# Turned tokens: from transposes on TensorE to a second read in turned layout, normalized in the value stage

## The chip, the cores and the metric

The kernel runs on one NeuronCore of a Trainium2 chip. A core has five engines with instruction streams of their own: TensorE (PE in the profile; its weight loads are PEld), VectorE (DVE), ScalarE (ACT), GpSimd (POOL) and SyncE (SP), which here issues nearly all DMA transfers. Each engine runs its stream in order, and engines wait for one another by semaphores. The metric is the device time of one execution in microseconds (us), lower is better; the time before is the median of three runs.

## The reference

One block of gated cross attention and a linear layer with adapters, over 32 sequences of 64 tokens of 512 elements, all in fp32 (shortened):

```python
def _layernorm(x, axis=-1, eps=1e-05):
    m = jnp.mean(x, axis=axis, keepdims=True)
    v = jnp.var(x, axis=axis, keepdims=True)
    return (x - m) / jnp.sqrt(v + eps)

# in attention: 32 heads of 128
q = (hidden_q @ Wq).reshape(b, lq, h, dh)
k = (hidden_kv @ Wk).reshape(b, lk, h, dh)
v = (hidden_kv @ Wv).reshape(b, lk, h, dh)
score = jnp.einsum('bqhd,bkhd->bhqk', q, k) * scale + position_bias
score = jnp.where(mask, score, neg_inf)
probs = jax.nn.softmax(score, axis=-1)
ctx = jnp.einsum('bhqk,bkhd->bqhd', probs, v).reshape(b, lq, h * dh)
return ctx @ Wo
...
x = x + jnp.tanh(g_xattn[0]) * attention(_layernorm(x), ctx_4096, mask, fside, Wq, Wk, Wv, Wo)
x = x + jnp.tanh(g_ffn[0]) * linear_with_adapters(_layernorm(x), ...)
```

The change touches one thing in it: `_layernorm(x)` of the first line, and the form in which it reaches the query product. That product contracts over the 512 elements, so it wants the normalized tokens turned: elements on the partitions, tokens along the free dimension.

## The kernel before

The tokens are handled in two phases (NPH = 2) of 1024 tokens (TP), each cut into NT = 8 tiles of 128 tokens and NCH = 2 halves of 512 tokens. A phase has three stages.

**Stage K** (the first loop of `stage_a`, line 619): for each of the 16 head pairs n, the product of the context with Wk. From n = 2 on, each is one `unit` (line 347): a 2 x 2 block product in seven products (p1 to p7) instead of eight, each product in three matmul passes over high and low halves of both operands (`mm3`). The operands are the high and low parts of the seven sums of blocks. For the weights `key_blocks` (line 533) makes them while the unit before runs: POOL forms sums and low parts, ACT the high parts, from `rawk`, which SP loads through `fetch`, two buffers in turn. ACT and DVE gather the products into `kT` (two buffers), and `store` sends it to DRAM (`kd`). A unit's last two products and its store are carried into the next unit.

**Stage V** (the second loop, line 661): for each of four groups g of weights and each of four token slices t, a `unit` with Wv; `store` sends the results to `vd`. The blocks of group g + 1 are made on POOL and ACT (`blocks_v`), from `wvr`, loaded at t = 1 of group g. In group 2 `turned_sums` starts, on POOL, to form the sums of the turned tokens `f`; in group 3 `turned_blocks` goes on with them.

**Attention** (`attention`, line 698) then runs over the head pairs with the query product, scores, softmax, probabilities times values, and the output product. After the second phase comes the linear layer.

The order of work is written out by hand. Side work runs in generators held in the list `streams`; `beat()` advances each by one step, and `unit` calls it after each of its seven products. `drain(g)` finishes a generator at once. Instructions go to their engines in the order in which this program reaches them. All loads and stores named here but two are on SP's queue, in order.

**The turned tokens before.** From n = 3 on `x_stats` (line 561) loads the eight token tiles (`xs`) and takes mean and variance with tokens on the partitions (bn_stats, bn_aggr); `ln_rstd` computes one over the root in small DVE steps. At n = 9 `x_turns` (line 574) starts: each tile is loaded again (`xt`), normalized on DVE (`ln_apply`, line 129: one tensor_scalar with a mean and a factor per partition), transposed on TensorE against the identity in four pieces into one PSUM buffer (`transposes`, line 132), and copied by ACT into the two tiles `f` (`x_turn`, line 520). The tiles `f` hold [128 elements, 4, 512 tokens] each, and take the slots in which the context lay. The stage ends with `drain(xturn)` and `drain(v0)`.

PSUM has eight buffers of 128 x 512 fp32 for everything. The tiles of tag "row" have two buffers of 128 x 512.

## Time and profile before

| what | value |
|---|---|
| median of three runs | 1547.89 us (1547.86 to 1548.68) |
| the profiled execution, its own time | 1547.98 us |
| its span, first to last instruction | 1545.8 us |
| granted TensorE clock, mean | 1.000 of full speed |
| stage K, first phase (0 to 162.7 us) | PE busy 161.26, DVE 98.80, ACT 78.44, POOL 120.14; DMA share 0.57 |
| stage V, first phase (162.7 to 327) | PE busy 164.30, DVE 69.16, ACT 56.54, POOL 121.84; DMA share 0.50 |
| stage K, second phase (724 to 895) | PE busy 171.00, DVE 111.82, ACT 81.18, POOL 127.94; DMA share 0.53 |
| stage V, second phase (895 to 1060) | PE busy 165.00, DVE 77.35, ACT 56.36, POOL 121.69; DMA share 0.50 |

How to read it: a busy time is the sum of an engine's instructions in the stretch; matmuls are pipelined, so that their durations overlap and a busy PE isn't PE at its peak. "DMA share" is the mean busy share of the core's 16 DMA engines. Matmuls and other groups are named by the tile they write and the tile they read, without buffer numbers ("tpx<-ident,xt"); Lnnn is a line of the kernel, often that of a helper. In a timeline the columns are start, length, engine, line, operation and tiles, and in brackets the idle time before and who ended it. The chain of work is followed back from the last instruction through whatever released each step.

### The profile page before, as it was taken

The page shows a single profiled execution, that of the slowest core. Times are in us where ns is not written, and L with a number is a line of the kernel's source. Part 1 is how long each engine was busy: PE and PEld are TensorE (multiplying, and loading weights), DVE is VectorE, ACT ScalarE, POOL GpSimd, SP SyncE. Part 2 cuts the span into 40 slices and gives each one's busy share as a digit, 9 for nine tenths or more (in the row PEclk, how much of TensorE's full clock was granted, in tenths as well). Part 3 has the DMA queues.
Part 4 walks back from the last instruction along what each step waited for, and adds up shares of the span by engine and source line. Part 5 has one row for each costly group of instructions (what it writes and reads, how often), then busy time and mean ns, then how long its engine had stood idle before and what let it go on. Part 6 is the DMA issues. An engine that isn't in the chain of part 4 may idle for free.

```text
span 1545.8 us, 24999 instructions
## 1 busy us (share of the span) xinstructions
PE 1538.4 (100%) x9080; PEld 1295.4 (84%) x9080; DVE 946.5 (61%) x1579; ACT 728.6 (47%) x1605; POOL 1015.8 (66%) x1128
## 2 busy tenths in 40 slices
PE   9999999999999999999999999999999999999999
PEld 7888888888888888888888888888888888888887
DVE  5675343377676757575686536437666676757763
ACT  6354233345555555556435423334555555555620
POOL 3898378967665757575589837896666665757410
PEclk9999999999999999999999999999999999999999
DMA  6654444374243424441565544438424342544201
GB/s 211 239 191 177 167 169 163 137 280 177 83 177 137 167 85 176 187 150 65 215 213 191 177 170 165 164 136 290 167 85 176 137 175 84 179 182 161 68 35 67
DMA packets 80989, 246.37 MB, mean 159 GB/s; under 512 B 9857, under 2 KB 10881, under 8 KB 72674
## 3 DMA queue, kind: packets, MB, share of 16 engines
q1 hardware_dynamic: 80578, 244.26, 43.9%
q8 instruction: 71, 1.16, 0.3%
q10 hardware_dynamic: 288, 0.52, 0.1%
q14 instruction: 52, 0.43, 0.1%
HBM read 171.35 MB, written 73.40 MB: 158 GB/s over the span
## 4 chain that ended last, share of the span: by engine, by line
PE 96%; DMA 2%; DVE 2%; issue 0%; ACT 0%; POOL 0%; SPq 0%; DVEq 0%; ACTq 0%; POOLq 0%
PE pa L96 22%; PE po L817 7%; PE pzv L96 6%; PE pvv L96 6%; PE pxv L96 6%; PE pzq L96 5%; PE pxq L96 5%; PE pxk L96 5%; PE pzk L96 5%; PE pvk L96 5%; PE pvq L96 5%; PE ps L759 4%; PE pf L96 4%; PE ppk L96 3%; PE pyv L96 3%; PE pyk L96 2%
## 5 line engine op out<-in xcount | busy, mean ns | idle before, releaser
L96 PE MATMUL pa<-wo,ch 128*128 128x512 f32 x1024 | 319.9, 393 | 0.0
L792 ACT COPY pt<-tp 32x256 f32<-32x256 f32 x496 | 200.3, 404 | 87.3 <-DVE tp L775 76.2
L88 POOL TENSOR_TENSOR wo<-rawo,wo 128x512 fp32r<-128x512 f32 x64 | 81.2, 1288 | 223.1 <-ACT wo L87 215.3
L96 PEld LDWEIGHTS pa<-wo,ch 128*128 128x128 f32 x1024 | 189.4, 188 | 40.0
L841 DVE TENSOR_TENSOR acc<-pa,acc 128x512 f32<-128x512 f32 x256 | 170.0, 673 | 79.5 <-PE pa L96 79.3
L96 PE MATMUL pa<-wo,cl 128*128 128x512 f32 x512 | 199.7, 390 | 0.0
L817 PEld LDWEIGHTS po<-pt,v 128*128 128x128 f32 x1024 | 119.1, 192 | 2.6 <-ACT pt L792 0.2
L821 DVE TENSOR_TENSOR cl<-po,ch 128x512 fp32r<-128x512 f32 x128 | 88.3, 691 | 51.9 <-ACT ch L820 51.4
L817 PE MATMUL po<-pt,v 128*128 128x128 f32 x1024 | 119.4, 275 | 0.0
L352 DVE TENSOR_TENSOR vt<-pvv,vt 128x512 f32<-128x512 f32 x64 | 44.1, 689 | 113.3 <-PE pvv L96 113.3
L96 PEld LDWEIGHTS pa<-wo,cl 128*128 128x128 f32 x512 | 96.1, 188 | 20.7
L820 ACT CAST ch<-po 128x512 fp32r<-128x512 f32 x128 | 75.0, 586 | 72.0 <-PE po L817 71.4
L765 ACT ACTIVATE sm<-sm 128x512 f32<-128x512 f32 x64 | 40.5, 633 | 122.7 <-POOL sm L764 122.7
L764 POOL TENSOR_TENSOR sm<-sm,mx 128x512 f32<-128x512 f32 x64 | 66.9, 1048 | 45.6 <-DVE mx L763 45.6
L374 ACT COPY vt<-pxv 128x512 f32<-128x512 f32 x32 | 18.8, 588 | 132.7 <-PE pxv L96 132.7
L352 DVE TENSOR_TENSOR kT<-pvk,kT 128x512 f32<-128x512 f32 x56 | 38.5, 688 | 69.4 <-PE pvk L96 68.8
L720 POOL TENSOR_TENSOR sm<-sm,madd 128x512 f32<-128x512 f32 x60 | 76.4, 1296 | 2.7 <-DMA sm<-bias 2.7
L783 POOL TENSOR_TENSOR sm<-sm,r 128x512 f32<-128x512 f32 x64 | 66.9, 1045 | 14.5 <-DVE r L782 11.1
L759 PE MATMUL ps<-kB,qT 128*64 128x64 f32 x2048 | 67.2, 224 | 0.3 <-DVE qT L352 0.3
L352 DVE TENSOR_TENSOR qT<-pzq,qT 128x512 f32<-128x512 f32 x64 | 44.2, 691 | 38.0 <-PE pzq L96 37.6
L352 DVE TENSOR_TENSOR vt<-pzv,vt 128x512 f32<-128x512 f32 x64 | 44.2, 691 | 37.1 <-PE pzv L96 36.9
L759 PEld LDWEIGHTS ps<-kB,qT 128*64 128x64 f32 x2048 | 62.5, 138 | 4.9 <-issue 0.7
(976 smaller groups left out, 3706.2 us busy)
## 6 DMA issues: line engine op xcount, KB each, us to landing
kd<-kT SPq DMA_DIRECT2D x64, 512.0 KB, 3.2
vd<-vt SPq DMA_DIRECT2D x128, 256.0 KB, 2.3
kB<-kd SPq DMA_DIRECT2D x32, 1024.0 KB, 4.9
v<-vd SPq DMA_DIRECT2D x32, 1024.0 KB, 8.7
rawq<-wq SPq DMA_DIRECT2D x32, 512.0 KB, 4.1
sm<-bias SPq DMA_DIRECT2D x64, 256.0 KB, 5.3
rawo<-wo SPq DMA_DIRECT2D x32, 512.0 KB, 3.5
rawk<-wk SPq DMA_DIRECT2D x31, 512.0 KB, 5.6
```

Of the source, the lines that this page charges most:

```text
L88: eng.tensor_tensor(lo, raw, hi.bitcast(F32), ALU.subtract)
L96: nc.tensor.matmul(ps, a, b, start=start and i == 0, stop=stop and i == 3 * n - 1, skip_group_check=True)
L352: nc.vector.tensor_tensor(o, ps, i, ALU.add)
L720: nc.gpsimd.tensor_tensor(t, t, masks[p][0], ALU.add)
L759: nc.tensor.matmul(ps[h * S:(h + 1) * S, t, :], qT[:, i, tok], kT[:, i, tok], start=True, stop=True)
L764: nc.gpsimd.tensor_tensor(s, s, mx.unsqueeze(2).to_broadcast([P, NT, S]), ALU.subtract)
L783: nc.gpsimd.tensor_tensor(ss[i], ss[i], r.unsqueeze(2).to_broadcast([P, NT, S]), ALU.mult)
L792: f(pt[dst, i, :, src], of[src, :, ki * 32:(ki + 1) * 32])
L817: nc.tensor.matmul(ps[:, t * P:(t + 1) * P], b["v", n // 2][c][:, t, hg * P:(hg + 1) * P], pt[:, i, c * 4 + t, :], start=True, stop=True)
L820: nc.scalar.copy(ch[:, i, sl], ps)
L821: nc.vector.tensor_tensor(cl[:, i, sl], ps, ch[:, i, sl].bitcast(F32), ALU.subtract)
L841: nc.vector.tensor_tensor(acc[t], ps, acc[t], ALU.add)
```

## The change

The host hands over a second copy of x, `xT`, in turned layout (per half of 512 tokens and quarter of 128 elements, [128 elements, 512 tokens]). Stage K reads it at n = 3 straight into `f`: eight loads of 256 KB, issued ahead of the first loads of wv. `x_turns` and `x_turn` go, with their second load of the token tiles, their normalizations on DVE, their transposes on TensorE and their copies on ACT.

The statistics are computed as before, with tokens on the partitions. In turned layout the mean and the factor of a token must stand on every partition, in the token's column. So `x_spread`, at n = 10, writes the 1024 means and the 1024 factors to DRAM (`lnd`), token by token, by two DMAs whose innermost runs on the DRAM side are single elements of 4 bytes; and `x_norm`, a stream of stage V's first group, reads them back as rows of 512 spread over all 128 partitions (`partition_broadcast`), two rows for each half, and subtracts and multiplies in place: 16 tensor_tensor of 128 x 512 on DVE in each phase, one per beat. It is drained when group 1 begins. The statistics are drained at n = 10 instead of n = 9.

```diff
@@ flamingo_block @@
+    lnd = [dram.tile([2, TP], F32, name=f"lnd{p}") for p in range(NPH)]
...
-    def x_turn(xt, f, p, t):
-        ps = transposes(xt, f"x{p}_{t}")
-        nc.scalar.copy(f[t // 4][:, :, (t % 4) * P:(t % 4 + 1) * P], ps)
...
-    def x_turns(p, f):
+    def x_spread(p):
         mv, y = mvx[p], rx[p]
-        xt = x_load(p, 0, "xt")
-        for t in range(NT):
-            nx = x_load(p, t + 1, "xt") if t + 1 < NT else None
-            for _ in range(2):
-                yield
-            ln_apply(xt, xt, mv, y, t)
+        nc.sync.dma_start(out=lnd[p][0].rearrange("(t q) -> q t", q=P), in_=mv[:, :, 0])
+        nc.sync.dma_start(out=lnd[p][1].rearrange("(t q) -> q t", q=P), in_=y)
+
+    def x_norm(p, f):
+        for j in range(NCH):
+            row = [rows.tile([P, 512], F32, tag="row", name=f"ln{p}_{j}_{i}") for i in range(2)]
+            for i in range(2):
+                nc.sync.dma_start(out=row[i], in_=lnd[p][i][j * 512:(j + 1) * 512].partition_broadcast(P))
             for _ in range(3):
                 yield
-            x_turn(xt, f, p, t)
-            xt = nx
-            yield
+            for op, r in ((ALU.subtract, row[0]), (ALU.mult, row[1])):
+                for kt in range(KT):
+                    nc.vector.tensor_tensor(f[j][:, kt, :], f[j][:, kt, :], r, op)
+                    yield
...
             if n == 3:
                 f = [big(f"f{j}", [P, KT, 512], F32, f"xf{p}_{j}") for j in range(2)]
+                for j in range(NCH):
+                    for kt in range(KT):
+                        nc.sync.dma_start(out=f[j][:, kt, :], in_=xT[p * NCH + j, kt])
...
-            if n == 9:
+            if n == 10:
                 drain(xstat)
-                xturn = x_turns(p, f)
-                streams.append(xturn)
+                x_spread(p)
...
-        drain(xturn)
         drain(v0)
+        xnorm = x_norm(p, f)
+        streams.append(xnorm)
         xq = {}
         for g in range(NG):
             if g == 1:
+                drain(xnorm)
                 streams.append(mask_stream(p))
...
         "x": C(A(x).reshape(ntok // P, P, D)),
+        "xT": C(A(x).reshape(NPH * NCH, 512, KT, P).transpose(0, 2, 3, 1)),
```

More of the change, by code (lines that the diff above doesn't have):

```diff
@@ L42, in flamingo_block @@
 @with_exitstack
-def flamingo_block(ctx: ExitStack, tc: tile.TileContext, x, ctxT, bias, mask, gx, gf,
+def flamingo_block(ctx: ExitStack, tc: tile.TileContext, x, xT, ctxT, bias, mask, gx, gf,
                    wq, wk, wv, wo, wffn, bffn, la, lb, starts, out):
```

## The prediction

> **What bounds the kernel now.** I read the page's busy times and its chain first.

> ```profile
> PE 1538.4 (100%) x9080; PEld 1295.4 (84%) x9080; DVE 946.5 (61%) x1579; ACT 728.6 (47%) x1605; POOL 1015.8 (66%) x1128
> ...
> PE 96%; DMA 2%; DVE 2%; issue 0%; ACT 0%; POOL 0%; SPq 0%; DVEq 0%; ACTq 0%; POOLq 0%
> ```

> TensorE (PE) is busy for 1538.4 of 1545.8 us and 96% of the chain. Work taken off PE shortens the time by what PE spent on it, provided that nothing newly late makes PE wait. The clock column stands at full speed throughout. Next, the instructions on the tile that the change removes:

> ```profile
> L135 PE MATMUL tpx<-ident,xt x64: 270/272/273, 100.4 to 894.0; 128*128 128x128 f32 x64
> ...
> L522 ACT COPY xf<-tpx x16: 577/587/593, 101.5 to 894.3; 128x512 f32<-128x512 f32 x16
> ```

> The 272 ns are a pipelined duration, not what a transpose takes from PE. That comes from the chain in order of time (start, length, what), where one unit starts after another:

> ```profile
> 81.49 2.72 PE pxk L96 x12
> 91.01 2.72 PE pxk L96 x12
> 100.97 2.77 PE pxk L96 x12
> ...
> 171.04 2.72 PE pxv L96 x12
> ...
> 823.79 2.72 PE pxk L96 x12
> ...
> 903.82 2.72 PE pxv L96 x12
> ```

> A unit without transposes takes 91.01-81.49 = 9.52 us. From 91.01 to 171.04 lie eight units with the eight token tiles' transposes: 80.03 us, not 8 x 9.52 = 76.16. The difference, 3.87 us (0.48 per tile), is the price; the second phase has the same 80.03 (823.79 to 903.82).

> [...] the 0.74 us POOL operation takes 1.20 beside a DVE one. [...] No store of single elements is in this trace. [...]

> **The change, part by part.**

> *Removed, stage K, each phase:* 8 x 4 transposes, 3.87 us of PE, so 7.74 us in all. Also 8 copies of 0.587 us on ACT, 8 normalizations on DVE (0.81 us) and 8 loads of 256 KB. These last three were off the chain: worth nothing by themselves.

> *Added at n = 3:* eight loads of the turned tokens, 2.1 MB, ahead of the wv loads. Eight issues of 0.44 us (four of ctx took 1.75) fit between 32.43, the end of a rawk issue, and 40.13, the next kd issue, with the four wv and two xs issues (3.2 us). The old contents of f0/f1 were last read near 24.4 us, so SP has no wait. But the data meets a full DMA:

> ```profile
> 34.00:46.50 12.50, 12.50 (x57) 10.36 (x56) 5.62 (x10) 5.31 (x15) 12.34 (x18) 1.00 1.01 375
> 103.50:109.00 5.50, 5.50 (x26) 4.51 (x25) 3.71 (x5) 2.43 (x6) 4.65 (x6) 1.00 0.07 22
> ```

> (Stretch, busy times, clock, DMA share, GB/s.) At 375 GB/s, 2.1 MB take 5.6 us; the rawk load at 41.02 lands that much later, and the key blocks behind it move:

> ```profile
> 41.02 0.71 SPq L262 DMA_DIRECT2D rawk<-wk  x1
> ...
> 47.47 0.41 ACT L293 CAST wk5p<-rawk 128x256 fp32r<-128x256 f32 x1 [0.53 <-DMA rawk<-wk]
> ...
> 53.07 0.74 POOL L297 TENSOR_TENSOR wk5p<-wsk,wk5p 128x256 fp32r<-128x256 f32 x1
> ...
> 54.40 0.66 DVE L190 TENSOR_TENSOR vs<-wvr_0a,wvr_0b 128x512 f32<-128x512 f32 x1
> ...
> 54.46 1.20 POOL L297 TENSOR_TENSOR wk5p<-wsk,wk5p 128x256 fp32r<-128x256 f32 x1
> ...
> 58.21 1.52 PE L96 MATMUL pyk<-c0p,wk5p 128*128 128x512 f32 x6
> ```

> The tightest block is p6: POOL ends its low part at 53.81, PE reads it with the third matmul of py, at 58.21+0.45 = 58.66. Late by 5.6, POOL ends at 59.4: PE waits 0.75. In the second phase the same part ends at 785.92 for 791.44: 0.1. DVE's bn_stats also waits up to 5 us for the xs load queued behind; the eight PSUM buffers hold a whole unit of results (9.5 us), so PE doesn't feel it. The kd stores come late too and hold ACT's copy into kT; ACT already waits for them at 46.35 and 56.68 for 0.65 and 1.46 us. Bounds for both phases together: 0 to 4 us; I take 0.8.

> *Moved, n = 9 to n = 10:* the wait for the statistics. They are on DVE before 97.7, where the first normalization uses them; no cost.

> *Added at n = 10:* two stores of 1024 separate 4-byte elements on SP's queue, behind the kd and rawk issues that end at 98.9. Behind them stand the kd store at 108.32 and the rawk load at 109.22. Between, the DMA is nearly empty (second row above, share 0.07): 5 us are free. The late rawk then has some 3.8 us before PE needs its block (p6 of block 12 ends at 121.9 and is read at 127.1; four transposes before that are gone, 1.9, and the kd store comes 0.5 sooner). So up to 8.8 us for the pair is hidden. The price isn't shown; the small reads bound it:

> ```profile
> DMA packets 150, 0.00 MB, mean 0 GB/s; under 512 B 150, under 2 KB 150, under 8 KB 150
> ...
> q1 hardware_dynamic: 150, 0.00, 4.9%
> ```

> (17.8 to 19.2 us, the 4-byte broadcasts of gx and gf.) In engine time that is 0.049 x 16 x 1.4 us / 150 = 7.3 ns each, in arrival 1.4/150 = 9.3 ns each. For 2048 elements: 0.9 us if all 16 engines run so, 19 us if they arrive as those did. Between stands the 192-byte read of la: 507 small packets within 1430.5 to 1431.5, 2 ns apart, 4 us for 2048. I take 4 us: hidden under the empty stretch. [...]

> *Added in stage V, group 0:* four row broadcasts of 256 KB each phase, and 16 tensor_tensor of 128x512 on DVE. One is about 0.69 us (DVE rows on SBUF: 0.66 to 0.69). [...] They make 11 us among 12.4 us of other DVE work in 38.08 us: room enough. The first two rows go out at the stage's first beat, when the DMA stands idle (share 0.00 from 165 to 168), and land before the third beat's end. All 16 operations are out by the 22nd of 28 beats, so the drain at g = 1 finds nothing. A broadcast costs 0.65 us at 400 GB/s, or 10.5 us if one engine of 16 carries it; I take 0.65. The first eight operations fall before 177.4, where POOL is idle, waiting for wv. The second eight meet POOL's blocks for group 1: 8 x 0.46 (1.20 less 0.74) = 3.7 us, less 1.3 us of POOL's own gaps before 203, leaves 2.4 late. The tightest block is p3:

> ```profile
> 207.27 2.73 POOL L186 TENSOR_TENSOR wv_1p<-vs,wv_1p 128x512 fp32r<-128x512 f32 x2
> ...
> 213.04 1.52 PE L96 MATMUL pzv<-wv_1p,c0p 128*128 128x512 f32 x6
> ```

> POOL ends at 210.0 and PE comes at 213.04: 3.0 us cover 2.4. Cost nothing; without that cover up to 2.4 a phase. turned_sums reads f only in group 2.

> **Sum.** The profiled execution took 1547.98 us (span 1545.8, 2.2 around it). 1547.98 - 7.74 + 0.8 = 1541.04; it lies 0.09 above the median of the runs, so against 1547.89 the forecast is **1541.0**.

> **The rivals.**
> 1. *The small DMAs crawl (slower).* If the element stores share few engines [...], the pair takes about 17 us (near the 19 above). Beyond 8.8 that is 8.2 us of late rawk and PE waiting, in each phase: 1547.98 - 7.74 + 16.4 = 1556.6; broadcasts on one engine would add to it. It decides from 8.8 + 3.87 = 12.7 us per pair, 6.2 ns per element. For it: the 9.3 ns arrivals. Against: [...] la at 2 ns, and the empty stretch.
> 2. *The burst at n = 3 costs more.* The late kd store blocks ACT, ACT the casts, and PE waits 2 to 3 us a phase: 1543 to 1546. For it: ACT is already held by kd there. Against: each block but p6 has 5 us or more to spare.
> 3. *POOL is late in stage V.* All 16 DVE operations collide: 16 x 0.46 - 1.3 - 3.0 = 3.1 a phase, so 1547.98 - 7.74 + 0.8 + 6.2 = 1547.2. For it: a slack of only 3.0. Against: POOL's 20.7 us wait for wv.
> 4. *Removed PE work gives nothing*, since some other wait takes the place: 1547.9. Against: PE has no idle time in this stage.

> **How the numbers follow.** Main case 0.64 (1539.5 to 1542.5); rival 1 0.14, rival 2 0.12, rival 3 0.08, rival 4 0.02. 0.2% is 3.1 us, about what a measurement tells from no change. Faster by more: 0.64, 0.10 of rival 2, 0.04 of rival 3, together 0.78; within: 0.08; slower: rival 1, 0.14. The range 1539.5 to 1549 holds all but rival 1; its lower end is the whole 7.74 with no new wait (1540.15) and a little for the scatter of the runs, and the DMA bounds up to 4 us lie within it.

> **What would show it.** Right: no tpx rows; units of 9.52 us through stage K to its end; a PE wait below 1 us near 58 us and none elsewhere; the two element stores landed before about 108; vt additions on DVE still following PE. Wrong: PE waits for key blocks from n = 11, behind late rawk loads; a DMA share near one, or one engine's worth, with few GB/s, between 99 and 120; POOL's wv_1p after PE wants it at 200 to 213; DVE waiting long for the row loads.

## The result and the profile after

The changed kernel takes 1549.88 us (median of 22 runs, 1547.44 to 1553.85) against 1547.90 for the kernel before (22 runs, 1547.61 to 1549.51): a ratio of 1.0013, 95% interval 1.0008 to 1.0019. The forecast was 1541.0, with a range from 1539.5 to 1549.0. The gain of 6.9 us that it promised is missing, and the kernel is 2.0 us slower than before. The runs of the changed kernel also spread over 6.4 us, where those of before spread over 1.9.

The profiled execution of the changed kernel happens to be its slowest, 1553.85 us (span 1552.1). So the experiments below hold a second profile of it, of 1548.46 us. First the page's busy times and the chain's shares by engine:

```profile
PE 1535.0 (99%) x9016; PEld 1291.1 (83%) x9016; DVE 978.7 (63%) x1595; ACT 718.8 (46%) x1589; POOL 1019.9 (66%) x1128
...
PE 93%; DMA 3%; DVE 2%; POOL 1%; issue 0%; SPq 0%; ACT 0%; DVEq 0%; ACTq 0%; POOLq 0%
```

TensorE issued 64 instructions less, as the change says, but is no longer busy all the time. What it waits for (us in total, times, longest), in the view of waits of TensorE:

```profile
PE pvk L97 <- DVE kT L353: 7.4, 2, 4.5
PE pvv L97 <- DVE vt L353: 1.9, 1, 1.9
```

Neither was there before. The two waits of the first line lie at n = 3 of the two phases, where the turned tokens are loaded. The timeline of phase 1 there (start, length, engine, line, operation; in brackets the idle time before and what ended it):

```profile
40.30 1.52 PE L97 MATMUL pvk<-c0p,wk3p 128*128 128x512 f32 x6
...
40.56 0.99 SPq L518 DMA_DIRECT2D xs<-x  x2
...
48.80 0.69 DVE L104 BATCH_NORM_STATS2 statsx<-xs 128x6 f32<-128x512 f32 x1 [7.55 <-DMA xs<-x]
...
49.62 0.66 DVE L353 TENSOR_TENSOR kT<-pvk,kT 128x512 f32<-128x512 f32 x1
...
50.43 2.90 PE L97 MATMUL pvk<-c0p,wk3p 128*128 128x512 f32 x6 [4.53 <-DVE kT L353]
```

Before, the same issues of `xs` stood at 34.45 and the same bn_stats ran at 42.73 after 1.25 us of waiting:

```profile
34.45 1.37 SPq L517 DMA_DIRECT2D xs<-x  x2
...
42.73 0.69 DVE L103 BATCH_NORM_STATS2 statsx<-xs 128x6 f32<-128x512 f32 x1 [1.25 <-DMA xs<-x]
...
43.56 0.66 DVE L352 TENSOR_TENSOR kT<-pvk,kT 128x512 f32<-128x512 f32 x1
...
45.97 1.52 PE L96 MATMUL pvk<-c0p,wk3p 128*128 128x512 f32 x6
```

What to see: the burst of eight `xT` loads stands ahead of the two `xs` loads on SP's queue, so the first token block arrives 6.07 us later (48.80 for 42.73). The transfer itself takes as long as before, 8.2 us from its issue to bn_stats; it is the issue that comes 6.11 us later (40.56 for 34.45), of which SP spends 3.7 us on issuing the eight loads. VectorE runs its stream in order, so the addition queued behind bn_stats (`kT<-pvk,kT`) is as late. That addition reads the PSUM buffer pv after product p7. TensorE's next use of pv is product p4, which accumulates onto the same buffer. Before, the addition ended at 43.56 + 0.66 = 44.22 and p4 began at 45.97. Less the 0.14 us that the chain shows between the two where TensorE waits, that leaves 1.6 us to spare. Late by 6.07, the addition makes 4.5 us of waiting; the trace has 4.53.

The wait costs more than its length. The stretches after it (columns: stretch, its length and PE busy, PEld, DVE, ACT, POOL busy, granted clock, DMA share, GB/s):

```profile
46.00:48.00 2.00, 0.00 (x0) 0.00 (x0) 0.00 (x0) 0.00 (x0) 1.48 (x3) 1.00 0.97 369
48.00:50.00 2.00, 0.00 (x0) 0.00 (x0) 1.17 (x3) 0.00 (x0) 0.00 (x0) 0.73 1.05 391
50.00:52.00 2.00, 1.57 (x4) 1.31 (x5) 1.75 (x4) 0.00 (x0) 0.00 (x0) 0.50 1.02 414
52.00:54.00 2.00, 2.00 (x7) 1.52 (x6) 0.63 (x1) 1.14 (x3) 0.07 (x1) 0.50 0.90 293
54.00:56.00 2.00, 2.00 (x7) 1.57 (x6) 0.13 (x2) 0.47 (x2) 2.00 (x3) 0.56 0.07 16
56.00:58.00 2.00, 2.00 (x10) 1.65 (x9) 1.97 (x4) 0.70 (x2) 1.84 (x4) 1.00 0.00 0
```

TensorE comes back at half its clock and stays there for some 5 us: products of 1.36 us take 2.90 and 2.56. The granted clock fell to 0.50 at 48.94 us, 3.0 us after the end of TensorE's last product before the wait (45.90), and was full again 6.83 us later. The last section sets this beside the other waits of these profiles.

Where the changed kernel's units run undisturbed, they do what was forecast. From the chain of the first profile, in the part of stage K where the transposes used to be:

```profile
98.06 2.72 PE pxk L97 x12
...
107.58 2.72 PE pxk L97 x12
```

9.52 us apart, where before a unit with a tile's transposes took about 10.0. So the gain is there, and the waits eat it.

### The profile page after: what moved, and what is told of

Same layout as the page of the kernel before. It is cut to its first block, busy times and chain, and to the rows that moved or that the text cites. A ratio compares the mean times of both kernels' runs of the same rounds, so it can differ in the third digit from the quotient of the medians.

```text
span 1552.1 us, 24867 instructions
## 1 busy us (share of the span) xinstructions
PE 1535.0 (99%) x9016; PEld 1291.1 (83%) x9016; DVE 978.7 (63%) x1595; ACT 718.8 (46%) x1589; POOL 1019.9 (66%) x1128
## 4 chain that ended last, share of the span: by engine, by line
PE 93%; DMA 3%; DVE 2%; POOL 1%; issue 0%; SPq 0%; ACT 0%; DVEq 0%; ACTq 0%; POOLq 0%
PE pa L97 22%; PE po L822 7%; PE pvv L97 6%; PE pzv L97 6%; PE pxv L97 6%; PE pzq L97 5%; PE pxq L97 5%; PE pvq L97 5%; PE pzk L97 5%; PE pvk L97 5%; PE pxk L97 4%; PE ps L764 4%; PE pf L97 4%; PE pyv L97 3%; PE pyq L97 3%; PE ppk L97 2%
## 5 line engine op out<-in xcount | busy, mean ns | idle before, releaser
L97 PEld LDWEIGHTS pa<-wo,cl 128*128 128x128 f32 x512 | 96.1, 188 | 20.7
L191 POOL TENSOR_TENSOR vs<-wvr,wvr 128x512 f32<-128x512 f32 x24 | 33.5, 1406 | 53.1 <-DMA wvr<-wv 53.1
```

Source lines behind the costliest of these rows:

```text
L97: nc.tensor.matmul(ps, a, b, start=start and i == 0, stop=stop and i == 3 * n - 1, skip_group_check=True)
```

## The experiments

**Theory A:** VectorE waits, in order, for the token block queued behind the burst; TensorE waits for VectorE and then runs at half clock. **Rivals:** the transposes' time was never to be had (B); the small stores or the row loads are the matter (C); the late key store and weight load hold ScalarE and GpSimd, as the forecast had it (D); the burst costs little by itself (E).

### The eight loads one by one

```diff
             if n == 3:
                 f = [big(f"f{j}", [P, KT, 512], F32, f"xf{p}_{j}") for j in range(2)]
-                for j in range(NCH):
-                    for kt in range(KT):
-                        nc.sync.dma_start(out=f[j][:, kt, :], in_=xT[p * NCH + j, kt])
...
+            if 4 <= n < 4 + NCH * KT:
+                j, kt = divmod(n - 4, KT)
+                nc.sync.dma_start(out=f[j][:, kt, :], in_=xT[p * NCH + j, kt])
```

> The changed kernel with its eight turned token loads moved from one burst at n=3 to one load ahead of each unit of n=4 to 11; nothing else differs. Theory A (VectorE, in order, waits for the first token block that queues behind the burst; TensorE waits for VectorE and then runs at half clock): TensorE has no wait between 30 and 60 us of either phase, the 6.1 and 4.8 us go, and the time is 1540 to 1542.5 us, some 6 to 7 under the kernel before. Rival B (TensorE doesn't gain by the transposes that went, other work fills their time): 1547 to 1549 us whatever the loads do. Rival C (the burst isn't the matter, but the stores of 1024 small elements at n=10 and the row loads are): within 1.5 us of the changed kernel, 1548.5 to 1551 us.

Measured: 1540.06 us (1539.86 to 1540.91); ratio to before 0.9951 (0.9937 to 0.9965). The view of TensorE's waits has no pvk and no pvv any more. The chain where the wait was:

```profile
43.32 2.72 PE pxk L97 x12
46.04 1.36 PE pvk L97 x6
47.40 1.36 PE pzk L97 x6
...
52.84 2.72 PE pxk L97 x12
```

No gap, full clock. Span 1538.0 against 1545.8: 7.8 us, where the removed transposes were put at 7.74. B and C fall. This kernel beats both.

### The burst behind the first two token blocks

```diff
             nx = x_load(p, t + 1, "xs") if t + 1 < NT else None
+            if t == 0:
+                for j in range(NCH):
+                    for kt in range(KT):
+                        nc.sync.dma_start(out=f[j][:, kt, :], in_=xT[p * NCH + j, kt])
```

(The loop of eight loads at n = 3 goes.)

> The changed kernel with the same burst of eight turned token loads at n=3, only issued a little later in it, behind the first two token blocks that the moments are taken from. The stores of the keys and the loads of the next weights stay behind the whole burst, as late as in the changed kernel. Theory A (VectorE waits in order for the token block): VectorE's wait falls from 7.5 to 1 to 2 us, TensorE waits under 1 us a phase, and the time is 1540 to 1543.5 us. Rival D (the late weight load and the late key store count, through ScalarE and GpSimd, as the forecast had it): no more than 2 us gained, 1547.5 to 1550.5 us.

Measured: 1542.16 us (1541.11 to 1542.83), ratio 0.9962 (0.9950 to 0.9975). The whole burst is still there; only two loads of 256 KB changed places with it. TensorE's one wait for VectorE in this stage:

```profile
PE pvk L97 <- DVE kT L353: 1.0, 1, 1.0
```

The weights are as late as ever, in the chain of the same kernel:

```profile
44.42 7.63 DMA rawk<-wk
52.05 0.02 issue
52.07 0.04 POOLq L298
```

They land 7.63 us after their issue, and GpSimd idles 6.17 us for them, as against 6.45 in the changed kernel and 1.31 with the late loads. TensorE loses 1.7 us in all (span 1539.7 against 1538.0; 2.1 by the medians). So the late weights and key stores aren't what the changed kernel loses by: rival D falls, as the main cause. The one wait of 1.0 us is the old link on a smaller scale: in phase 2 the third token block now stands behind the burst, and VectorE waits 3.9 us for it, where 1 to 2 were expected.

### The burst alone, in the kernel before

The transposes stay; only these lines are added (and the array `xT`):

```diff
                 f = [big(f"f{j}", [P, KT, 512], F32, f"xf{p}_{j}") for j in range(2)]
+                for j in range(NCH):
+                    for kt in range(KT):
+                        nc.sync.dma_start(out=f[j][:, kt, :], in_=xT[p * NCH + j, kt])
```

> The kernel before, its transposes and row layout all kept, with only the burst of eight turned token loads added at n=3; what they load is overwritten later by the transposes' results, so the loads are pure addition. Theory A: TensorE waits 4 to 5 us in phase 1 and 3 in phase 2 and runs at half clock for some us after; the time is 8 to 11 us over the kernel before, 1556 to 1559 us. Rival E (the burst takes the place of something that the change also moved, and costs little by itself): 1548 to 1551 us.

Measured: 1558.34 us (1557.75 to 1558.47), ratio 1.0067 (1.0055 to 1.0080), 10.5 us more. The view of waits and the chain:

```profile
PE pvk L96 <- DVE kT L352: 6.4, 2, 3.5
```

```profile
38.74 8.29 DMA xs<-x
...
47.97 0.59 DVE kT L352
48.55 0.14 issue
48.69 2.19 PE pvk L96 x6
50.88 2.39 PE pzk L96 x6
53.26 1.38 PE pyk L96 x6
```

The burst makes the same wait and the same slow products with nothing else of the change present. Rival E falls. The change is about the sum of the two: -7.8 and +10.5 make +2.7, and the changed kernel shows +2.0.

### No normalization

From the kernel with the late loads, `x_spread` and `x_norm` and their calls are left out.

> The kernel with the late loads and without the two small stores, the row loads and the sixteen normalizing operations of each phase: the queries' tokens stay unnormalized, so this part of the computation is left out. It shows what the normalization by way of DRAM costs in all. Theory A (stores hidden behind TensorE's unit queue; only the stage of values of phase 2 loses 2.2 us to GpSimd's delay): 1.5 to 2.5 us below the kernel with the late loads. Rival F (it costs nothing, all hidden): within 0.7 us of it. Rival C (small stores are the matter): 5 us or more below it.

Measured: 1539.72 us (1539.59 to 1540.04), 0.34 below the kernel with the late loads. The two element stores, the four row loads and the sixteen VectorE operations of each phase are hidden almost wholly, as F expects. That I expected 1.5 to 2.5 us under A was a miss: it took the 1.9 us in the stage of values for a fixed cost.

### Half the burst

```diff
             if n == 3:
+                for kt in range(KT):
+                    nc.sync.dma_start(out=f[0][:, kt, :], in_=xT[p * NCH, kt])
...
             if n == 5:
+                for kt in range(KT):
+                    nc.sync.dma_start(out=f[1][:, kt, :], in_=xT[p * NCH + 1, kt])
```

> The changed kernel with four of the eight turned token loads at n=3 and the other four at n=5: half the dose in one place. Theory A by the traces so far (TensorE waits for what VectorE's wait exceeds about 3 us, then runs at half clock if the wait was 3 us or more): four loads delay the first token block by 2.8 to 3.1 us instead of 6.1, so TensorE waits 0 to 1.5 us a phase and the clock stays full; 1540 to 1543.5 us. If a wait grows in proportion to the burst (no cover): half of what the burst costs, 1544.5 to 1546 us.

Measured: 1541.69 us (1540.58 to 1544.05), ratio 0.9960 (0.9947 to 0.9972). The waits and the chain:

```profile
PE pvk L97 <- DVE kT L353: 1.2, 1, 1.2
```

```profile
37.02 8.55 DMA xs<-x
...
47.22 1.63 PE pvk L97 x6
48.85 1.38 PE pzk L97 x6
50.23 1.36 PE pyk L97 x6
```

Half the dose costs 1.6 us over the late loads, where the whole costs 9.8. The first token block is 2.86 us late here (bn_stats at 45.59 for 42.73); less the 1.6 us that VectorE had to spare, that makes 1.25 us of waiting, and the view has 1.2. A wait of 1.2 us brought no half clock (in the profiles till then it had followed waits of 2.9 to 4.5 us). Both bends make the cost grow faster than the dose.

### VectorE's first moments operation a unit later

The burst stays where it is, and every transfer up to TensorE's wait keeps its place (the token loads from the third on, which follow VectorE's operation, come later):

```diff
-            for _ in range(3):
+            for _ in range(3 if t else 10):
                 yield
             ln_moments(xt, mv[:, t, :], f"x{p}_{t}")
```

> The changed kernel with its burst and every transfer in the same order, and only one thing moved: VectorE's first moments operation of each phase comes ten beats behind its load instead of three, so it stands a unit later in VectorE's order. Theory A (the place of one waiting instruction in VectorE's order makes the loss, not the lateness of any transfer): VectorE waits under 1 us for the token block, TensorE 0 to 1.5 us a phase, no half clock; 1540 to 1543.5 us. Rival D (ScalarE is held by the late key store, over 6 us in the changed kernel's trace, and would hold TensorE by itself): TensorE waits 2 us or more a phase, now for ScalarE, 1544 to 1549 us.

Measured: 1542.75 us (1540.46 to 1545.09), ratio 0.9961 (0.9947 to 0.9975). The timeline of its profiled execution (1545.09 us, the slowest of the five):

```profile
47.44 0.69 DVE L353 TENSOR_TENSOR kT<-pvk,kT 128x512 f32<-128x512 f32 x1 [3.39 <-PE pvk L97]
...
51.85 0.59 ACT L358 COPY kT<-pxk 128x512 f32<-128x512 f32 x1 [6.24 <-DMA kd<-kT]
...
53.08 0.68 DVE L104 BATCH_NORM_STATS2 statsx<-xs 128x6 f32<-128x512 f32 x1
...
60.52 1.20 PE L97 MATMUL pyk<-c0p,wk5p 128*128 128x512 f32 x4 [0.90 <-POOL wk5p L298]
```

bn_stats now finds its data there, the additions follow TensorE, and the 4.5 us are gone. So the place of one waiting instruction in VectorE's order made the loss; ScalarE is held 6.24 us by the key store, about as long as in the changed kernel (6.32), and TensorE doesn't feel it. What is left, 0.90 us at py of block 5, is the wait that the forecast named: p6's low part on GpSimd, late by `rawk`. It was put at 0.75 and 0.1; here the views show 0.90 and 0.71. By the start of the products that follow, phase 1 is 2.1 us behind the kernel with the late loads (this block's pv begins at 61.55 for 59.48 in the timelines; 0.7 of it comes at p1, whose block the forecast had given 5 us to spare), and phase 2 1.0 more (791.47 for 788.39). The size was low, the place right. The remaining 2.2 us of this profile, whose span is 1543.3 against 1538.0, are a wait in the stage of values, which the next test is about.

### The small operations of the accumulators later

In the first profile of the changed kernel a 4-element operation on VectorE took 7.25 us beside GpSimd's weight blocks, and TensorE waited 1.94 us behind it. Two timelines, of the changed kernel and of the one with the late loads:

```profile
941.21 7.25 DVE L116 TENSOR_SCALAR yf<-vf 128x4 int32<-128x4 int32 x1
```

```profile
929.28 0.97 DVE L116 TENSOR_SCALAR yf<-vf 128x4 int32<-128x4 int32 x1
```

In the test the burst stays, and only `acc_rstd` starts a group later:

```diff
             if g == 1:
...
-                if p:
-                    streams.append(acc_rstd(p - 1))
...
+            if g == 2 and p:
+                streams.append(acc_rstd(p - 1))
```

> The changed kernel with its burst kept, and only the small operations that follow from the accumulators' moments of phase 1 begun at g=2 instead of g=1 of phase 2's stage of values. In the profile of the changed kernel one of them took 7.25 us beside GpSimd's run of weight blocks and TensorE waited 1.9 us behind it. Theory G (that wait recurs in most executions): 1.5 to 2.5 us under the changed kernel, 1547.4 to 1548.4 us, and no wait of TensorE in that stage. Theory H (it belongs to that one execution, which was the slowest of 22): no change against the changed kernel, 1549 to 1551 us. In both TensorE still waits at n=3 of both phases.

Measured: 1550.08 us (1547.66 to 1551.96, 21 runs), ratio to before 1.0012 (1.0006 to 1.0019), the same as the changed kernel. So this wait isn't in the usual execution (H). The second profile of the changed kernel says the same:

> The changed kernel itself once more, for a second profile. Theory A: TensorE waits 2 to 5 us at n=3 of either phase and half clock follows. Theory G: the 1.9 us of the stage of values of phase 2 are there again; theory H: they aren't. 1547.5 to 1553.5 us.

Measured: one run, 1548.46 us. Its waits and chain:

```profile
PE pvk L97 <- DVE kT L353: 6.3, 2, 3.3
```

```profile
39.50 8.32 DMA xs<-x
...
49.48 1.62 PE pvk L97 x6
51.10 2.56 PE pzk L97 x6
53.66 1.78 PE pyk L97 x6
...
783.29 1.63 PE pvk L97 x6
784.91 1.39 PE pzk L97 x6
```

No wait in the stage of values. It came back once more, with 7.25 us and 1.9 us, in the profiled execution with the moments a unit later: so it stands in two of the eight profiles of the changed kernel and its variants that keep these operations in their place. When it comes and when not is left open.

### The element stores twice

From the kernel with the late loads, each of the two stores is made twice, the second time to rows that nothing reads (`lnd` has four rows):

```diff
+        nc.sync.dma_start(out=lnd[p][2].rearrange("(t q) -> q t", q=P), in_=mv[:, :, 0])
+        nc.sync.dma_start(out=lnd[p][3].rearrange("(t q) -> q t", q=P), in_=y)
```

> The kernel with the late loads and with each of the two stores of 1024 elements of 4 bytes made twice, the second time to rows of the buffer in DRAM that nothing reads: the dose of small elements doubled. By the traces one pair keeps the transfers behind it back for some 10 us, which TensorE doesn't feel. If the forecast's break-even holds (8.8 us hidden per phase), two pairs, 20 us, cost 11 us a phase: 1558 to 1566 us. If other work covers more (the next key weights are there two units ahead), under 3 us in all: 1540 to 1543 us.

Measured: 1553.90 us (1553.77 to 1555.60), ratio 1.0040 (1.0027 to 1.0052): 13.8 us over one pair, between my two numbers but much nearer the high one. The waits, and the stretches of phase 1 (columns as above):

```profile
PE pxk L97 <- ACT kT L358: 8.9, 2, 4.8
```

```profile
112.00:116.00 4.00, 4.00 (x19) 3.32 (x18) 1.38 (x2) 0.00 (x0) 1.29 (x2) 1.00 0.87 26
116.00:120.00 4.00, 3.20 (x15) 2.31 (x13) 0.00 (x0) 0.00 (x0) 0.00 (x0) 1.00 0.83 80
120.00:124.00 4.00, 0.00 (x1) 0.01 (x1) 0.02 (x1) 0.59 (x1) 0.00 (x0) 0.65 0.99 351
124.00:128.00 4.00, 4.00 (x9) 3.13 (x10) 3.10 (x5) 1.54 (x4) 2.83 (x4) 0.50 0.66 250
```

The DMA engines are busy and move next to nothing: from 104 to about 120 us for 4096 elements, 3.9 ns each; with one pair, in the kernel with the late loads, it is from 104 to about 113 for 2048, 4.4 ns each. One pair, 9 to 10 us, stays hidden. The second lengthens the time by 8.9 us of waiting and some 5 of half clock. The link is the one of n = 3 with other names: the late key store holds ScalarE, whose copy must have read px before p2 accumulates onto it. So the transfers have a cover of about 11 us (16 less the longest wait of 4.8), and one pair uses up most of it.

## Why the prediction was wrong

**The step that failed** is in the paragraph on n = 3: "DVE's bn_stats also waits up to 5 us for the xs load queued behind; the eight PSUM buffers hold a whole unit of results (9.5 us), so PE doesn't feel it." The first half was right in kind (7.55 us of waiting, 6.3 of them new, most of it SP's late issue and not, as reckoned, data that meets a full DMA). The second was not. A number of buffers is a cover only where the next product takes a fresh one. In `unit`, p4 accumulates onto pv and p3 onto pz, and VectorE has to read pv with p7 in it before p4 may start. The cover was the time between that addition and p4, 1.6 us in the rows of the kernel before, not 9.5. Both rows were there to be read.

The wait so missed was about 3 to 4.5 us a phase, and half clock after it had no place in the sum at all. The books close on spans, against the kernel with the late loads (1538.0); each stretch is the shift of one product (the first pxk or pxv of the chain after the wait) against the same product there:

| | second profile (1546.7) | first profile (1552.1) |
|---|---|---|
| n = 3, phase 1 | 58.15 - 52.84 = 5.3 | 59.98 - 52.84 = 7.1 |
| n = 3, phase 2 | 790.38 - 781.75, less 5.3 = 3.3 | 793.68 - 781.75, less 7.1 = 4.8 |
| stage V, phase 2 | 952.22 - 943.60, less 8.6 = 0 | 957.71 - 943.60, less 11.9 = 2.2 |
| sum | 8.6 of 8.7 | 14.1 of 14.1 |

What sets the two columns apart is the length of the waits, whether the clock drops behind them (in phase 2 it stayed full after 3.0 us in the second profile and fell after 2.9 in the first), and the one wait in stage V. The mean granted clock on record for each of the 22 runs goes with their time (0.999 in the five fastest, 0.996 in the slowest), so half clock has a share in the spread; how long the waits of the other runs were isn't shown.

**Removed transposes, 7.74 us:** right; 7.8 came out once nothing else was in the way.

**Late weight blocks, 0.8 us:** the place was right, the size low (about 3 us in the one profile that shows it bare, inside the bounds of 0 to 4).

**Element stores, 4 us a pair, hidden up to 8.8:** the size was off by more than two (9 to 10 us, over 4 ns an element instead of the 2 that was the forecast's estimate), the verdict held, by a cover of about 11 us that was also larger than I had put it. The 2 ns from the read of la was too low by about the factor by which the 9.3 ns from the 4-byte reads, the high end, was too high.

**Normalization in stage V, nothing:** right (0.34 us with stores, row loads and all). The row loads landed 3.9 to 6.0 us after their issue in the first profile, not the 0.65 that was taken, an estimate, and not one engine's 10.5, and the operations took 1.09 us each in the median, not 0.69; TensorE hardly felt either.

**The rivals.** Rival 2 had the place and named the wrong hand: it looked at ScalarE behind the late key store, and asked which weight block would be late. It gave 1543 to 1546 without the clock. Rival 1 (the stores crawl) is what the doubled stores show, but a single pair doesn't reach it. Rival 3 came true in part: TensorE waited in stage V, but behind one small VectorE operation, and in some executions only. As a sign of being right I had named a TensorE wait below 1 us near 58 us and none elsewhere; the wait for VectorE at 46 us was on no list.

## What to carry to other kernels

For every load added ahead of others on a queue, list who waits for those others, and what stands behind the waiting instruction on its in-order engine; the cover is then the time from that engine's next read of a buffer to the next product that accumulates onto the same buffer, not the number of buffers. A burst that costs 9.8 us in one place cost nothing as eight loads in eight units, so spread a transfer over the stage before judging the change that needs it. Where TensorE is the bound, don't price a new wait at its length alone: here the clock fell to half behind eight waits of 2.9 to 4.8 us, and they cost 1.5 to 1.9 times their length.
